# Seven block products for eight in two pairs of row tiles, and a batch's column term added by GpSimd

## The chip, the cores and the metric

The kernel runs on one core of one Trainium2 chip. The metric is device time in microseconds of one execution, from the start to the end on the chip. Names of the engines in the profile: PE is TensorE's matmul, PEld its weight load, DVE is VectorE, ACT is ScalarE, POOL is GpSimd, SP is the sync engine, which here issues most DMAs.

## What is computed

Two blocks follow each other, each with a residual. The input `x` is 2 x 1024 x 2048 in f32, the context is 2 x 2048 x 2048, the weight 2048 x 2048.

```python
def xattn(x1, x2):                       # x1: layer norm of x, x2: the context
    q1 = fake_quant(x1, x1_scale, x1_zp) # round, clip to 0..255, less zero point, times scale
    q2 = fake_quant(x2, x2_scale, x2_zp)
    return q1 @ q2
def ffn(x, weight):
    s = 127 / clip(max(abs(x), axis=-1), 1e-5)
    xq = clip(round(x * s), -128, 127) / s
    scale_w = 1 / clip(mean(abs(weight)), 1e-5)
    tw = clip(round(weight * scale_w), -1, 1)          # -1, 0 or 1
    return einsum('bsi,oi->bso', xq, tw) / scale_w
x = x + tanh(g_xattn) * xattn(layernorm(x), context)
x = x + tanh(g_ffn) * ffn(layernorm(x), weight)
```

## The kernel before

**Tiling.** Each of the two batches is eight row tiles of 128 rows, held as f32 in `resid` (eight buffers, so that a row of batch 1 takes the buffer of a row of batch 0 once that is stored). Each batch has a first product (rows by context) and a second one (rows by weight), each 8 tiles x 2048 x 2048. A matmul is 128 x 128 by 128 x 512; half a row tile (1024 columns) of one product is 32 of them.

**First product** (`first`, L611, added to the row by VectorE at L620). The row is normalized (bn_stats L378), quantized by ScalarE (L434), clipped by VectorE (L437) and transposed into `turned` or `tw`, by PE in batch 0 (L444, copies L450) and by DMA on the SP queue in batch 1 (L454). The context is quantized into the f16 store `ca` by ScalarE (L547), clipped by VectorE (L550) and summed by columns (L555, L557, then PE at L581). Since the quantized values are kept centred, the zero points leave a **column term** `colg` (one value for each column, made by `column_term`, L586) and a **row term** `rowg` (one value for each row, summed in batch 0 by GpSimd at L460 to L465 and ScalarE at L469, in batch 1 by ScalarE at L473). `terms` adds both to the row in one VectorE instruction, which also gives the row's sum for the mean:

```python
nc.vector.scalar_tensor_tensor(                                    # L640
    v, colg, rowg[:, t : t + 1], v, ALU.add, ALU.add, accum_out=acc[:, i : i + 1])
```

**Second product** (`norm2`, `norm2_tile`, `second`). From the sum come the mean (L668), the squares and their sum (ScalarE, L677), the largest square (VectorE, L684), a few small operations on two rows at a time (L690 to L704, the root on ScalarE at L697, the product's scale `am` at L708), the quantization (ScalarE, L748), a cast (VectorE, L757) and the transposition (PE at L762 with copies at L768 for one pair, DMA at L774 for the others). PE multiplies with the ternary weight in fp8 (L814), VectorE scales and adds (L823), and the half row is stored (L829), issued by GpSimd, for the last two rows by SP.

**Weight.** The 16 tiles of the weight are loaded twice (L854): once for the mean of absolute values (L865, scale at L874 to L883), once for the quantization by ScalarE (L899), the clip to fp8 by VectorE (L903) and the transposition into `tw`, by PE and a copy for the first six (L909, L913), by DMA for the others (L917).

**Order.** No instruction is placed by hand. Each piece of work is a step in a `Plan`, with engine, cost in us, due time, the keys that it reads and writes, and flags for buffers, DMA time and `port`. `Plan.order` simulates the steps, at each turn taking the one that can start first on its engine, with the due time as a tie-break; `Plan.latest` goes back from the end and gives new due times; after ten such rounds the best order is issued. Two steps with `port` do not overlap in this simulation; it stands for what VectorE and GpSimd share. Engines work through their instructions in the order issued. The rows are taken in the order 6, 7, 0, 1, 2, 3, 4, 5, in batch 1 as 14, 15, 8 to 13. PSUM has three buffers `mm` of 1024 f32 columns for the products, and two `tr`. Five buffers `turned` hold transposed rows of either product.

In batch 1 the first products are written as column half 0 of four rows, half 1 of the same, then both halves of each of the last four; the second products follow row by row. The planner mixes them.

Of the kernel before, what the change touches and what calls it, by code (L numbers as in the profile page):

```python
# [18 lines left out]
Q_EPS = 1e-5  # L19
# [4 lines left out]
class Plan:  # L24
# [128 lines left out]
    def give_out(self):  # L153
# [6 lines left out]
        due, best = [s[2] for s in steps], None  # L160
        for i in range(self.ROUNDS):
            order, ends, passed = self.order(due, follow, waits)
            if best is None or max(ends) < best[0]:
                best = (max(ends), order)
            due = self.latest(ends, passed, follow)
        for n, slot in best[1]:
            if slot is None:
                steps[n][3]()
            else:
                steps[n][3](slot)  # L170
# [3 lines left out]
def flamingo_gated_kernel(  # L174
# [69 lines left out]
    acc = const.tile([P, MT], F32, name="acc")  # L244
    rowg = const.tile([P, 2 * MT], F32, name="rowg")
# [46 lines left out]
    plan = Plan({"work": NWORK, "tp": NTP, "mm": 3, "tr": 2})  # L292
    step = plan.step
    aT, qT, pm = {}, {}, {}
    taken = {}

    def scalars():

        s = {}

        def spread(slot):
            s["pp"] = tr[slot]
            nc.tensor.matmul(s["pp"][:, 2:6], ones32[0:1, :], par1[:, 2:6], start=True, stop=True)
            nc.tensor.matmul(s["pp"][:, 0:2], ones32[0:1, :], tg1, start=True, stop=True)

        def of(i, rs, zc):
            nc.vector.reciprocal(rs, par[:, i : i + 1])  # L310
            nc.vector.tensor_scalar(zc, par[:, i + 1 : i + 2], CENTER, None, ALU.subtract)

        def rest():
            nc.vector.scalar_tensor_tensor(g1, par[:, 2:3], par[:, 4:5], tg[:, 0:1], ALU.mult, ALU.mult)
            nc.vector.scalar_tensor_tensor(g1d1, zc1, -1.0, g1, ALU.mult, ALU.mult)
            nc.vector.scalar_tensor_tensor(g1d2, zc2, -1.0, g1, ALU.mult, ALU.mult)
            nc.vector.tensor_scalar(kd2, zc2, -float(K), None, ALU.mult)
            nc.vector.tensor_scalar(gkd, kd2, g1d1, None, ALU.mult)

        step("ACT", 0.3, 0.0, lambda: nc.scalar.activation(tg1, par1[:, 0:2], AF.Tanh), wr=[("tg1",)], hold=4.0)  # L320
        by = step("PE", 0.6, 6.0, spread, rd=[("tg1",)], wr=[("pp",)], take="tr", hold=6.8)
        step(
            "DVE", 0.2, 6.0, lambda: nc.vector.tensor_copy(par, s["pp"][:, 0:6]), rd=[("pp",)],
            wr=[("par",)], give=[by],
        )
        step("DVE", 0.3, 6.1, lambda: of(2, rs1, zc1), rd=[("par",)], wr=[("p1",)])
        step("DVE", 0.3, 6.2, lambda: of(4, rs2, zc2), rd=[("par",)], wr=[("p2",)])
        step("DVE", 0.9, 10.0, rest, rd=[("p1",), ("p2",)], wr=[("g",)])

    def res(t):  # L330
        return resid[:, t % MT, :]

    def xk(t, h=None):
        return [("x", t % MT, i) for i in ((0, 1) if h is None else (h,))]

    strip = const.tile([P, 30 * 2 * MT], F32, name="strip")
    stats6 = const.tile([P, 4, K // 512, nc.vector.BN_STATS_DIM], F32, name="stats6")
    used = [0]

    def tiny(n=1):  # L340
        used[0] += n
        return strip[:, used[0] - n : used[0]]


    def load_x(t, due, queue, halves=1, hold=0.0):
        w = K // halves
        for h in range(halves):

            def bring(h=h):
                q = nc.sync if queue == "SP" else nc.gpsimd  # L350
                q.dma_start(out=res(t)[:, ts(h, w)], in_=xrow[t][:, ts(h, w)])

# [67 lines left out]
    def norm1_tile(t, due, by_pe, fold_it, place, pieces, ready, scales, on_dve):  # L420
# [5 lines left out]
        def quant(i, slot=None):  # L426
            if i == 0:
                s["q"] = work[:, slot, :]
# [696 lines left out]
```

## Time and profile before

| | us |
|---|---|
| median of 3 runs | 498.72 (497.08 to 500.88) |
| profiled execution, its own time | 496.74 |
| its span | 495.0 |
| PE busy | 467.6 (2422 instructions) |
| DVE busy | 340.6 |
| ACT busy | 276.6 |
| POOL busy | 63.5 |

The span is the time from the first to the last instruction of the profiled execution; busy times are shares of it. In the profile's lines L611 is line 611 of the kernel. A group's line gives the engine, the operation, written tile and read tiles, shape, count, then busy time and the mean of one in ns, then the idle time of the engine just ahead of those instructions and what ended it. By the chain of waits the first matmuls run from 25 us, the first product of batch 0 until about 146, its second product until 274, mixed at its end with batch 1's first product, whose last pieces lie at 427, and the rest is the second product of batch 1. Batch 0's eight L640 lie between 113 and 162, batch 1's between 346 and 432.

### The profile page before, as it was taken

The numbers are of one execution on the slowest core, as the hardware profiler recorded it, in microseconds if no ns is written. First come the engines' busy times: TensorE is split into PE (matmuls) and PEld (weight loads), VectorE is DVE, ScalarE is ACT, GpSimd is POOL, SyncE is SP. The second block draws the span as 40 slices with busy tenths as digits, with TensorE's granted clock in tenths as the row PEclk, the third lists the DMA queues.
The fourth block names the chain that finished last, engine by engine and source line by source line (L and its number), as shares of the span: only waits on it lengthen the run. The fifth ranks groups of instructions, "written<-read, shape, count | busy, mean of one in ns | idle before, by whom it ended". The sixth has DMA issues, their size and how long they took to land.

```text
span 495.0 us, 6179 instructions
## 1 busy us (share of the span) xinstructions
PE 467.6 (94%) x2422; PEld 223.0 (45%) x2422; DVE 340.6 (69%) x568; ACT 276.6 (56%) x258; POOL 63.5 (13%) x76
## 2 busy tenths in 40 slices
PE   0599999999998799999999999999999999999996
PEld 0244454444467344444444444444444444444442
DVE  4999989959999688556697957632989831572122
ACT  4997896878999988631488364530454430050000
POOL 0574529100000020100100100000000000000000
PEclk9999999999999899999999999999999999999999
DMA  8999968992189999999999995610041542215122
GB/s 293 425 419 424 366 214 338 428 407 81 60 215 366 260 301 295 306 258 330 402 363 341 297 269 189 100 28 1 0 66 47 144 111 102 86 61 153 79 92 85
DMA packets 76170, 108.94 MB, mean 220 GB/s; under 512 B 58220, under 2 KB 58220, under 8 KB 70892
## 3 DMA queue, kind: packets, MB, share of 16 engines
q1 hardware_dynamic: 72064, 93.86, 60.1%
q0 software_dynamic: 4064, 14.68, 7.7%
q8 instruction: 19, 0.31, 0.2%
q14 instruction: 11, 0.09, 0.1%
q10 hardware_dynamic: 12, 0.00, 0.0%
HBM read 77.59 MB, written 16.78 MB: 191 GB/s over the span
## 4 chain that ended last, share of the span: by engine, by line
PE 76%; DVE 14%; DMA 6%; issue 2%; ACT 1%; DVEq 0%
PE mm L814 40%; PE mm L611 32%; DVE resid L640 3%; DMA resid<-in_x_dram 2%; PE tr L814 2%; DVE strip L684 2%; DMA tw<-in_ctx_dram 2%; DVE resid L620 2%; DMA tw<-ca 2%; DVE stats L378 1%; DVE ca L550 1%; DVE ca L903 1%; ACT ca L547 1%; PE tr L444 1%; DVE colg L557 1%
## 5 line engine op out<-in xcount | busy, mean ns | idle before, releaser
L814 PE MATMUL mm<-tw,turned 128*128 128x512 fp8e4 (+1 forms) x1104 | 211.9, 353 | 4.7 <-DMA turned<-work 2.4
L611 PE MATMUL mm<-ca,turned 128*128 128x512 f16 x832 | 187.7, 384 | 0.5 <-DVE ca L550 0.3
L814 PEld LDWEIGHTS <-turned 128*128 128x128 f16 x1168 | 106.8, 98 | 122.7 <-issue 6.3
L611 PEld LDWEIGHTS <-turned 128*128 128x128 f16 x832 | 81.8, 99 | 99.0 <-issue 4.8
L823 DVE SCALAR_TENSOR_TENSOR resid<-mm,am,resid 128x1024 f32<-128x1024 f32 (+1 forms) x31 | 38.6, 1246 | 64.3 <-PE mm L814 64.2
L547 ACT ACTIVATE ca<-ca,scal 128x2048 int16<-128x2048 f32 (+1 forms) x30 | 50.5, 1692 | 36.9 <-DMA ca<-in_ctx_dram 36.4
L677 ACT ACTIVATE work<-resid,strip 128x1024 f32<-128x1024 f32 x32 | 36.4, 1138 | 57.8 <-DVE strip L668 54.1
L829 POOL DMA_DIRECT2D out_dram<-resid x30 | 18.1, 606 | 362.5 <-DVE resid L823 225.2
L620 DVE SCALAR_TENSOR_TENSOR resid<-mm,scal,resid 128x1024 f32<-128x1024 f32 x32 | 40.4, 1277 | 18.4 <-PE mm L611 18.2
L378 DVE BATCH_NORM_STATS2 stats<-resid 128x6 f32<-128x512 f32 x64 | 40.0, 678 | 7.9 <-DMA resid<-in_x_dram 7.9
L550 DVE TENSOR_SCALAR ca<-ca 128x2048 f16<-128x2048 int16 (+1 forms) x40 | 27.3, 698 | 24.5 <-ACT ca L547 24.5
L611 PE MATMUL mm<-ca,tw 128*128 128x512 f16 x192 | 43.1, 379 | 0.4 <-DVE tw L450 0.2
L748 ACT ACTIVATE work<-resid,strip 128x2048 int16<-128x2048 f32 x16 | 35.5, 2263 | 12.2 <-DVE strip L704 7.8
L684 DVE TENSOR_REDUCE strip<-work 128x1 f32<-128x1024 f32 x32 | 37.3, 1210 | 1.3 <-ACT work L677 1.3
L640 DVE SCALAR_TENSOR_TENSOR resid<-colg,rowg,resid 128x2048 f32<-128x2048 f32 x16 | 37.4, 2344 | 0.1
L434 ACT ACTIVATE work<-resid,strip 128x2048 int16<-128x2048 f32 (+1 forms) x17 | 33.4, 1984 | 1.3 <-DVE strip L400 1.3
L557 DVE TENSOR_TENSOR colg<-colg,ca 128x2048 f16<-128x2048 f16 x24 | 30.8, 1304 | 0.3
L611 PEld LDWEIGHTS <-tw 128*128 128x128 f16 x192 | 18.4, 98 | 22.8 <-DVE tw L450 0.7
L899 ACT ACTIVATE work<-ca,scal 128x2048 int16<-128x2048 f32 x13 | 25.6, 2005 | 1.6 <-DMA ca<-in_L_ffn_weight_dram 1.1
L473 ACT ACTIVATE work<-work,scal 128x2048 f16<-128x2048 f16 x8 | 16.0, 1994 | 18.5 <-DMA turned<-work 18.5
L865 ACT ACTIVATE tw<-ca 128x2048 int8<-128x2048 f32 x10 | 19.1, 1910 | 7.6 <-DMA ca<-in_L_ffn_weight_dram 7.5
L462 POOL TENSOR_TENSOR tw<-tw,work 128x512 f16<-128x512 f16 x16 | 21.8, 1364 | 1.6 <-DVE work L437 0.4
(93 smaller groups left out, 260.7 us busy)
## 6 DMA issues: line engine op xcount, KB each, us to landing
ca<-in_L_ffn_weight_dram SPq DMA_DIRECT2D x19, 1024.0 KB, 8.6
ca<-in_ctx_dram SPq DMA_DIRECT2D x16, 1024.0 KB, 12.3
resid<-in_x_dram SPq DMA_DIRECT2D x15, 1024.0 KB, 11.7
out_dram<-resid POOLq DMA_DIRECT2D x26, 512.0 KB, 3.8
tw<-in_ctx_dram SPq DMA_DIRECT2D x8, 1024.0 KB, 12.6
ca<-in_ctx_dram SPq DMA_DIRECT2D x14, 512.0 KB, 8.4
tw<-in_L_ffn_weight_dram SPq DMA_DIRECT2D x6, 1024.0 KB, 6.8
out_dram<-resid SPq DMA_DIRECT2D x3, 512.0 KB, 2.6
```

Source lines behind the costliest of these rows:

```text
L378: nc.vector.bn_stats(stats6[:, t % 4, c, :], res(t)[:, ts(c, 512)])
L434: nc.scalar.activation(d, v, AF.Identity, bias=bi, scale=sc)
L547: nc.scalar.activation(a.bitcast(I16), s["w"], AF.Identity, bias=zc2, scale=rs2)
L557: nc.vector.tensor_add(r, r, a2(kt - kt % 2, h * H, 2 * H))
L611: nc.tensor.matmul(pm[t][:, ts(q, U)], aT[t][:, kt, :], a2(kt, h * H + q * U, U), start=(kt == 0), stop=(kt == KT - 1),)
L620: nc.vector.scalar_tensor_tensor(v, pm[t], g1, v, ALU.mult, ALU.add)
L640: nc.vector.scalar_tensor_tensor(v, colg, rowg[:, t : t + 1], v, ALU.add, ALU.add, accum_out=acc[:, i : i + 1])
L677: nc.scalar.activation(s["dev", t, h], res(t)[:, ts(h, H)], AF.Square, bias=s["nm"][:, j : j + 1], accum_out=s["s2"][:, k : k + 1],)
L684: nc.vector.tensor_reduce(s["m2"][:, k : k + 1], s["dev", t, h], AX.X, ALU.max)
L748: nc.scalar.activation(s["q"].bitcast(I16).rearrange("p (k j c) -> p k j c", j=2, c=P), v.rearrange("p (k c j) -> p k j c", j=2, c=P), AF. ...
L814: nc.tensor.matmul(pm[t][:, o + b0 * P : o + b1 * P], qT[t][:, k, j, :], w8[:, k, j, b0 * P : b1 * P], start=(k + j == 0), stop=(k + j == PB),
L823: nc.vector.scalar_tensor_tensor(v, pm[t][:, 0 : n * U], am[:, t : t + 1], v, ALU.mult, ALU.add)
```

## The change

**Seven for eight.** For the last two pairs of rows in batch 1 (10 with 11, and 12 with 13), the second product of a pair is taken as a product of 2 x 2 blocks: a block row for each tile, the inner dimension and the columns cut in halves of 1024. `seven` does it with seven block products of 16 matmuls, over sums and differences of row blocks (`sums`, VectorE, f16) and differences of weight blocks (`weight_differences`, GpSimd, fp8, written where the context's column half 0 lay in `ca`). The parts accumulate in PSUM buffers x, y and z, and are added to the rows on the way (`take`), y being read and then accumulated further. The pairs before keep `second`.

**Terms of batch 0.** `terms` in batch 0 becomes four GpSimd additions of the column term, 512 columns each; the row's sum comes from the accumulator of the addition in `first` and from a new `column_sum`; the row term is left out until after the second product, where ScalarE adds it to each half row before the store.

**With it.** In batch 1 rows from the third on are normalized one by one (`alone`, `var_alone`, `scale_alone`), no more in pairs. The last four weight tiles are quantized by VectorE (`on_dve`). The last two rows' first products go half 0, half 0, half 1, half 1. The plan is made twice: all steps up to batch 1's products keep the due times found for the version without `seven`.

The body of the kernel moved into a function `build(SEVEN)`, which indents it; without that the core of the diff is:

```diff
         def add():
-            nc.vector.scalar_tensor_tensor(v, pm[t], g1, v, ALU.mult, ALU.add)
+            o = dict(accum_out=part_acc[:, 2 * t + h : 2 * t + h + 1]) if t < MT else {}
+            nc.vector.scalar_tensor_tensor(v, pm[t], g1, v, ALU.mult, ALU.add, **o)
...
+    def column_sum(due):
+        def go():
+            nc.vector.tensor_reduce(csum, colg, AX.X, ALU.add)
+            nc.vector.tensor_scalar(csum, csum, -1.0 / N, None, ALU.mult)
+        step("DVE", 2.45, due, go, rd=[("colg", 0), ("colg", 1)], wr=[("csum",)])
     def terms(t, due):
...
+        if t < MT:
+            for c in range(NQ):
+                step(
+                    "POOL", 1.3, due, lambda c=c: nc.gpsimd.tensor_add(v[:, ts(c, U)], v[:, ts(c, U)], colg[:, ts(c, U)]),
+                    rd=[("colg", c // 2)], wr=xk(t, c // 2), port=True,
+                )
+            return
...
         def mean(j, t):
+            if t < MT:
+                a = [part_acc[:, 2 * t + h : 2 * t + h + 1] for h in range(2)]
+                nc.vector.tensor_scalar(m, a[0], a[1], -1.0 / N, ALU.add, ALU.mult)
+                nc.vector.tensor_scalar(m, m, csum, None, ALU.add)
...
     def second(t, h, due, parts, pool="mm", last=False, apart=False):
...
+        if t < MT:
+            step(
+                "ACT", 0.3 + 0.45 * n, due + 2.0,
+                lambda: nc.scalar.activation(v, v, AF.Identity, bias=rowg[:, t : t + 1]),
+                rd=[("rowg", t)], wr=keys,
+            )
...
+    HK = PB // 2
+    def weight_differences(dues, engines):
+        for i, (due, by) in enumerate(zip(dues, engines)):
+            for q in range(2):
+                b11, b12, b21, b22 = w_part(q, 0), w_part(q + 2, 0), w_part(q, 1), w_part(q + 2, 1)
+                pair = ((b12, b11), (b22, t_part(0, q)), (b22, b12), (b21, t_part(1, q)))[i]
...
+                for c in range(PIECES[by]):
+                    def go(i=i, q=q, by=by, pair=pair, at=ts(c, w)):
+                        eng = nc.vector if by == "DVE" else nc.gpsimd
+                        eng.tensor_tensor(
+                            t_part(i, q)[:, at], pair[0][:, at], pair[1][:, at], ALU.subtract, saturate=False
+                        )
+                    step(
+                        by, w * (1.05e-3 if by == "DVE" else 2.35e-3) + 0.1, due, go, rd=rd, wr=[t_key(i, q)],
+                        port=True,
+                    )
+    PIECES = {"DVE": 4, "POOL": 8}
+    ENGINES = ("POOL",) * 4
+    def seven(pair, i, due, last):
...
+        def sums(n):
+            if n == 0:
+                nc.vector.tensor_add(s1, flat[u][:, 0:half], a22())
+            elif n == 1:
+                nc.vector.tensor_sub(s2, s1, a11())
+            elif n == 2:
+                nc.vector.tensor_sub(flat[u][:, 0:half], a11(), flat[u][:, 0:half])
+            else:
+                nc.vector.tensor_sub(s4, a12(), s2)
...
+        product("y", a11, lambda q: w_part(q, 0), lambda q: qt + W4(q, 0), due, start=True)
+        take("y", t, 0, due + d)
+        product("x", a12, lambda q: w_part(q, 1), lambda q: qt + W4(q, 0), due + d, start=True)
+        store(t, 0, take("x", t, 0, due + 2 * d, give=True), due + 2 * d)
+        product("y", lambda: s2, lambda q: t_part(1, q), lambda q: [keys[1]] + tk(1)(q), due + 2 * d)
+        take("y", t, 1, due + 3 * d)
+        product("z", lambda: s1, lambda q: t_part(0, q), lambda q: [keys[0]] + tk(0)(q), due + 3 * d, start=True)
+        take("z", u, 1, due + 4 * d)
+        product(
+            "y", lambda: flat[u][:, 0:half], lambda q: t_part(2, q), lambda q: [keys[2]] + tk(2)(q), due + 4 * d,
+        )
+        store(u, 1, take("y", u, 1, due + 5 * d), due + 5 * d)
+        product("z", lambda: s4, lambda q: w_part(q + 2, 1), lambda q: [keys[3]] + W4(q, 1), due + 5 * d)
+        store(t, 1, take("z", t, 1, due + 6 * d, give=True), due + 6 * d)
+        for q in range(2):
+            product(
+                "y", a22, lambda q: t_part(3, q), lambda q: qu + tk(3)(q), due + 6 * d, qs=(q,), give=give,
+            )
+            if last:
+                store(u, 0, take("y", u, 0, due + 7 * d, q == 1, q), due + 7 * d, q)
...
-        weight_quant(ot, place[ot], due, ot < 8 or ot % 2 == 1, ot > 5)
+        weight_quant(ot, place[ot], due, ot < 8 or ot % 2 == 1, ot > 5, ot >= 12)
...
-    plan.give_out()
+    plan, before = build(0)
+    due = plan.rounds()[0][:before]
+    plan, _ = build(2)
+    plan.give_out(plan.rounds(due)[1])
```

## The prediction

> **What bounds the kernel now.** I read the page first, then the chain of waits in order of time, then the timelines of the engines around the places where TensorE (PE) stands still. Busy share, granted clock and the chain's shares by engine:
>
> ```profile
> PE 467.6 (94%) x2422; PEld 223.0 (45%) x2422; DVE 340.6 (69%) x568; ACT 276.6 (56%) x258; POOL 63.5 (13%) x76
> ...
> PEclk9999999999999899999999999999999999999999
> ...
> PE 76%; DVE 14%; DMA 6%; issue 2%; ACT 1%; DVEq 0%
> ```
>
> PE is busy for 94% of the span at full clock but for one slice, and it holds 76% of the chain. DVE's 14% lies almost wholly before and in the handover from the first to the second product of batch 0. The chain in time (start, length, what):
>
> ```profile
> 161.37 7.80 DMA tw<-ca
> 169.17 0.14 issue
> 169.31 12.21 PE mm L814 x48
> ...
> 184.97 10.36 PE mm L814 x48
> ...
> 428.43 62.17 PE mm L814 x288
> 490.60 0.03 issue
> 490.63 0.75 DVE resid L823
> ```
>
> The last stretch is one unbroken row of 288 matmuls in 62.17 us: 215.9 ns for each, with nothing between. From 169 us on the chain is PE alone (column sums included), so there **a matmul less is 0.216 us less, as long as its operands come in time**. What else can move lies before: PE's timeline at the handover (start, length, and in brackets the idle time before it and its releaser):
>
> ```profile
> 153.60 2.85 PE L814 MATMUL mm<-tw,turned 128*128 128x128 fp8e4 x48 [2.35 <-DMA turned<-work]
> ...
> 163.36 3.61 PE L814 MATMUL tr<-tw,turned 128*128 128x512 fp8e4 x16 [1.10 <-ACT turned L768]
> 169.31 12.21 PE L814 MATMUL mm<-tw,turned 128*128 128x512 fp8e4 x48 [2.33 <-DMA tw<-ca]
> ```
>
> PE stands 2.35 + 1.10 + 2.33 = 5.78 us, and after the last gap 48 matmuls took 12.21 us where the same 48 took 10.36 us at 184.97: 1.85 us more, at a granted clock of 0.91 in the window 160 to 180. Together 7.63 us are there to be won or enlarged.
>
> **The seven products.** A pair of row tiles costs 8 block products of 16 matmuls now, 7 after the change; two pairs: 2 x 16 x 215.9 ns = **6.91 us off PE**, in the last stretch, where PE is the whole chain. The number of matmuls per weight load is unchanged. The end of the last matmul moves from 490.6 to about 483.7, and the two pairs take 2 x 7 x 3.454 = 48.4 us, so pair one begins near 435.3. By its order its third product (442.2) needs the first and second weight difference, the fifth (449.1) the third, the seventh (456.0) the fourth.
>
> **The weight differences.** New: 64 GpSimd subtractions of 512 fp8 elements, two inputs. No fp8 operation on GpSimd is in the trace. The nearest rows are the fp16 adds of 512 elements, two of them alone, the first undisturbed and the second beside VectorE's column adds (L557):
>
> ```profile
> 59.76 1.15 POOL L460 TENSOR_TENSOR tw<-work 128x512 f16<-128x512 f16 x1 [4.15 <-DVE work L437]
> ...
> 79.50 2.13 POOL L460 TENSOR_TENSOR tw<-work 128x512 f16<-128x512 f16 x1
> ```
>
> So the price lies between 1.15 and 2.13 us; the 24 adds of L460 and L462 took 11.9 + 21.8 = 33.7 us, 1.40 each, and I take that (same operation, same width, a like mix of neighbours). 64 x 1.40 = 90 us. They may start when all first products with column half 0 of batch 1 have passed. Those run from 260.9, with 32 matmuls of L814 and some 6 of column sums mixed in; half 0 of the last two rows is written after 12 units of 32 matmuls, so it is complete after 12 units if PE takes it early (384 + 38 matmuls, 352) and 14 units if it takes them as written (366). I take 359. Stores that GpSimd issues in between (8 x 0.53 for the four plain tiles, L829) add 4 us. The fourth difference ends at 359 + 90 + 4 = 453, 3 us ahead of 456. Cost **0, with little to spare**: the cover is the 55 us of plain products between. At 1.15 us it ends at 437; at 2.13 at 499, 43 us late.
>
> The Trainium skill, "SBUF — State Buffer", section "Who interferes with whom", speaks against this placing: a VectorE instruction with two SBUF inputs, or in a two-port mode, and a GpSimd instruction that reads SBUF exclude each other for the whole instruction. The pair of lines above agrees in kind (1.15 against 2.13). By that rule 64 x 1.15 would grow by five L640 of 2.34 us and eight casts of 0.69 us that lie after 359: 91 us, ending at 454, no other verdict than the mean row gives.
>
> **VectorE in the pairs.** Seven takes a pair instead of four, 1.28 each (L823): +3.8 us. Four sums of 1024 fp16 elements; L557 does 2048 in 1.30, so 0.65 each: +2.6 us. Six tiles are now normalized alone: 17 small operations a tile instead of 6, near 0.2 us each: 13 us over the stretch. By the windows VectorE is busy for 80 of the 155 us after 340; it would be for about 100 after the change, so it fits in sum. What it can cost is a late take, because the next product but one accumulates in the same buffer. The slack shows in
>
> ```profile
> 452.64 1.28 DVE L823 SCALAR_TENSOR_TENSOR resid<-mm,am,resid 128x1024 f32<-128x1024 f32 x1 [5.31 <-PE mm L814]
> 456.09 1.28 DVE L823 SCALAR_TENSOR_TENSOR resid<-mm,am,resid 128x1024 f32<-128x1024 f32 x1 [2.17 <-PE mm L814]
> 466.45 1.28 DVE L823 SCALAR_TENSOR_TENSOR resid<-mm,am,resid 128x1024 f32<-128x1024 f32 x1 [9.08 <-PE mm L814]
> ```
>
> the 2.17 us that VectorE waits between the adds of two units. A take behind one L640 (2.34 us) is late by 0.2, behind a sum held by a GpSimd operation (0.65 + 1.15) by nothing. Bounds 0 to 2 us (a few of 14 takes late by 0.2 to 0.5); **+0.5**.
>
> **The column term on GpSimd.** Eight additions L640 go from VectorE in batch 0 (8 x 2.34 = 18.7 us, all between 113 and 162, where it is busy without a break), 32 GpSimd adds of 512 f32 come (no f32 add there in the trace; bounds again 1.15 and 2.13, at 1.40: 5.6 us a tile, 45 in all), plus the accumulator reads (16 x 0.08), a reduce of the column term (two L684 of 1.21: 2.4 us) and a second small operation per mean. Net VectorE falls by some 14 us. GpSimd has been idle since 88, and the column term's half 0 is there at 103.1, so half 0 of the first tiles is hidden; half 1 is there at 113.1 and takes 2.3 to 4.3 us a tile against 2.34 now. The groups:
>
> ```profile
> L823 DVE SCALAR_TENSOR_TENSOR resid<-mm,am,resid 128x1024 f32<-128x1024 f32 (+1 forms) x31 | 38.6, 1246 | 64.3 <-PE mm L814 64.2
> ...
> L677 ACT ACTIVATE work<-resid,strip 128x1024 f32<-128x1024 f32 x32 | 36.4, 1138 | 57.8 <-DVE strip L668 54.1
> ...
> L640 DVE SCALAR_TENSOR_TENSOR resid<-colg,rowg,resid 128x2048 f32<-128x2048 f32 x16 | 37.4, 2344 | 0.1
> ...
> L462 POOL TENSOR_TENSOR tw<-tw,work 128x512 f16<-128x512 f16 x16 | 21.8, 1364 | 1.6 <-DVE work L437 0.4
> ```
>
> What is that worth at the handover? ScalarE (ACT) is as full as VectorE there: from 117.94 to 162.3 it idles 1.8 us, and its squares, quantizations and copies stay. But VectorE's queue did hold things up: ScalarE ended the quantization of a weight tile at 155.29,
>
> ```profile
> 153.25 2.04 ACT L899 ACTIVATE work<-ca,scal 128x2048 int16<-128x2048 f32 x1
> ```
>
> and VectorE, in an L640 begun 0.1 us before, clipped it only at 157.46:
>
> ```profile
> 155.19 2.34 DVE L640 SCALAR_TENSOR_TENSOR resid<-colg,rowg,resid 128x2048 f32<-128x2048 f32 x1
> ...
> 157.46 2.35 DVE L903 TENSOR_SCALAR ca<-work 128x2048 fp8e4<-128x2048 int16 x2
> ```
>
> These 2.2 us stand ahead of the weight transposes on the SP queue (issued from 158.74) that PE waited for at 169.3. They share the DMA with five weight loads issued at 150.1, so not all of it comes through. Bounds: a gain of 7.63 (all idle time and slow clock gone); a loss of 2.3 us, where at 2.13 us an add the third tile (three tiles of half 1: 113.1 + 3 x 4.26 = 125.9) is late for its second square, which ScalarE started at 123.59. Nearer to the single hold-up, half of which is hidden by DMA: **-1.0**.
>
> **The row term on ScalarE.** 16 activations of 1024 f32 at the end of batch 0, 1.14 each (L677): 18.2 us, less four weight quantizations of 2.0 us that go to VectorE (no f32 to int16 on VectorE in the trace: between 0.69, L757, and 2.34, L640; 1.22 as L903, 4.9 us in all). ScalarE is busy 76.8 of the 120 us from 160 to 280 and would be 87. Each store goes out some 1.2 us later, and with it the load of batch 1's row that reuses the buffer. Cost 0: PE never idles from 182 on, the last such row was transposed by about 322 and first products for others lasted to 373. If that cover were gone, it would be about 1.2 us once, plus a wait behind context quantizations that wait for DMA (up to 5 us each). I add **+0.5** for it and for VectorE waiting at GpSimd's adds.
>
> **Sum.** -6.91 + 0 + 0.5 - 1.0 + 0.5 = -6.9 us, on the profiled execution of 496.74 (span 495.0 and 1.74 around it): 489.8. That execution was 2.0 below the median of the runs, 498.72, which is what is predicted from: **491.8 us**. A measurement here tells about 1% (5 us) from no change.
>
> **Rivals.** *The handover closes* (0.13): VectorE's freed time lets weights and rows through early, PE does not stop and keeps its clock: 498.7 - 6.9 - 7.6 + 1.0 (the two terms of 0.5) = 485.2. For it: three waits, one traced to an L640. Against: ScalarE is as full, DMA too.
> *Given back* (0.26): the subtractions cost 1.56 each, so the fourth difference ends at 359 + 100 + 4 = 463 and the seventh product waits 7 us: 498.7. For it: only 3 us to spare, and VectorE's L640 and casts in that stretch. Against: PE may take half 0 early (352).
> *GpSimd becomes the bound* (0.19), the slower side: fp8 subtraction at 1.77, half way between mean and contended rows. 64 x 1.77 = 113, end at 476, 20 us late: 498.7 - 6.9 + 20 = 511.9. It decides the sign from 1.56 us on ((456 + 6.9 - 363) / 64) and makes the kernel slower by over 1% from 1.64 (5 us more). For it: nothing in the trace prices fp8 there. Against: 1.15 undisturbed, and no column adds (L557) this late.
> That the change does not do what it says would show as a matmul count that is not lower by 32.
>
> **Numbers.** The forecast (0.42) has its own range of 488 to 494.5. Faster by over 1% (below 493.7): nearly all of it and the first rival, 0.54. Within 1%: given back and the rest, 0.27. Slower: 0.19. The range leaves out most of the slow rival and the far end of the first: 485 to 502.
>
> **What would show it.** Right: PE's instructions down by 32; the last stretch an unbroken row ending near 484; POOL busy up by about 135 us (45 + 90) with a mean near 1.4; the fourth difference done before the seventh product; gaps between 150 and 170 of 3 to 6 us. Wrong: PE waits for POOL in the last 50 us (GpSimd is the bound), POOL means above 1.6, or gaps at the handover longer than 5.8 us.

## The result, and the profile after

The changed kernel takes **527.72 us** (median of 4 runs, 522.95 to 530.77) against 499.8 us for the kernel before, run beside it on the same chip: a ratio of 1.0569, with a 95% interval of 1.0437 to 1.0701. Forecast were 491.8 us in a range of 485 to 502. The profiled execution took 530.61 us with a span of 528.7; before the span was 495.0, so 33.7 us are to be found.

The page of the changed kernel, the rows that answer to those of before (busy time, granted clock by slice, the chain's shares):

```profile
PE 471.1 (89%) x2390; PEld 223.4 (42%) x2390; DVE 408.5 (77%) x662; ACT 287.6 (54%) x275; POOL 176.4 (33%) x172
...
PEclk9999999999969999999999989999999969989999
...
PE 36%; DMA 25%; DVE 25%; ACT 7%; issue 4%; SPq 2%; POOL 0%; DVEq 0%; ACTq 0%; POOLq 0%
```

The matmuls went down by 32 as they should, yet PE's busy time went up by 3.5 us: seven products took off 6.9, which by subtraction leaves 10.4 to the lower granted clock (two slices of 6 and two of 8, where before had a single 8). PE's share of the chain fell from 76% to 36%; VectorE's went from 14% to 25% and the DMA's from 6% to 25% (42 us of it are two loads of the context between 12 and 55 us, before most of the new work). **GpSimd, which has most of the new work, holds 0% of the chain.** PE's idle time (span less busy) rose from 27.4 to 57.6 us, by 30.2. By windows 4.7 of these lie before 60 us, 9.3 between 140 and 200, 2.1 near 310, and 13.7 between 420 and 500; the rest is spread. PE's timeline where it now stands longest in the last two stretches (start, length, and in brackets the idle time before it and its releaser):

```profile
152.36 1.04 PE L1138 MATMUL tr<-ident,ca 128*128 128x128 f16 x8 [8.83 <-DVE ca L1132]
...
430.12 27.28 PE L879 MATMUL mm<-tw,turned 128*128 128x512 fp8e4 x112 [7.37 <-DVE resid L888]
...
461.57 6.21 PE L1005 MATMUL mm<-tw,turned 128*128 128x512 fp8e4 x16 [4.17 <-DMA turned<-work]
...
487.17 3.46 PE L1005 MATMUL mm<-ca,turned 128*128 128x512 fp8e4 x8 [2.12 <-DVE resid L1028]
```

The three gaps of the handover (2.35, 1.10 and 2.33 before) have become one of 8.83, two of 2.36 and 2.97 and two small ones, and the last stretch, unbroken before, has three. All the lines shown but one name VectorE; the one that names a DMA waited for a row whose transposition was issued only after a late VectorE cast. So the next view is VectorE's timeline around these places:

```profile
127.94 1.28 DVE L637 SCALAR_TENSOR_TENSOR resid<-mm,scal,resid 128x1024 f32<-128x1024 f32 x1
...
129.14 1.22 DVE L721 TENSOR_REDUCE strip<-work 128x1 f32<-128x1024 f32 x1
130.27 11.55 DVE L748 TENSOR_TENSOR strip<-strip 128x2 f32<-128x2 f32 x1
...
407.54 18.39 DVE L674 SCALAR_TENSOR_TENSOR resid<-colg,rowg,resid 128x2048 f32<-128x2048 f32 x1
...
428.79 1.28 DVE L888 SCALAR_TENSOR_TENSOR resid<-mm,am,resid 128x1024 f32<-128x1024 f32 x1
...
445.59 11.04 DVE L821 CAST work<-work 128x2048 f16<-128x2048 int16 x2
...
476.52 9.40 DVE L989 TENSOR_TENSOR ca<-turned,ca 128x1024 f16<-128x1024 f16 x1
```

The first two lines are a product's addition and a reduction, as long as ever. Then comes an operation on 128 x 2 numbers with two inputs, 0.15 us elsewhere, that took **11.55**; an L674 (the former L640, 2.34 us undisturbed) that took 18.39; two casts of 0.69 that took 11.04; and a sum of `seven` that took 9.40 instead of 0.69. The line at 428.79 is the L888 that ended PE's wait at 430.12: it stood in VectorE's queue behind the instruction of 18.39 us. GpSimd's timeline at the same times:

```profile
114.76 27.05 POOL L668 TENSOR_TENSOR resid<-resid,colg 128x512 f32<-128x512 f32 x22 [1.14 <-DVE colg L602]
...
416.38 7.40 POOL L961 TENSOR_TENSOR ca<-tw 128x512 fp8e4<-128x512 fp8e4 x7
...
476.90 8.46 POOL L961 TENSOR_TENSOR ca<-tw,ca 128x512 fp8e4<-128x512 fp8e4 x8
```

The first line is 22 adds of the column term without a gap, from 114.76 to 141.81; VectorE's 11.55 us end at 141.82. The second is the last 7 of 16 differences that began at 406.90 and ended at 423.78; VectorE's L674 ended at 425.93, its own 2.1 us later. The third ended at 485.36, VectorE's sum at 485.92. The casts stood beside a row from 444.89 to 455.47. So **on each of these four held lines VectorE stood until a whole row of GpSimd instructions was over, not until the one that was running was over.** It was not so everywhere: an L674 at 387.65 waited for a single difference and took 3.18 us. The instructions that were held read two SBUF tensors or are casts between 16-bit types; the additions that read PSUM (L637, L888, L1028) and the reductions of one tensor (L721) ran beside the same rows at full speed.

GpSimd's own work was about as dear as forecast, or less (busy time and mean ns after the bar):

```profile
L961 POOL TENSOR_TENSOR ca<-tw 128x512 fp8e4<-128x512 fp8e4 x32 | 37.2, 1193 | 77.4 <-PE mm L627 77.4
...
L668 POOL TENSOR_TENSOR resid<-resid,colg 128x512 f32<-128x512 f32 x32 | 44.9, 1447 | 37.8 <-DVE colg L602 21.2
...
L961 POOL TENSOR_TENSOR ca<-tw,ca 128x512 fp8e4<-128x512 fp8e4 x32 | 34.6, 1108 | 0.1
```

The 64 differences cost 37.2 + 34.6 = 71.8 us, 1.12 each, where 1.40 was taken, and the 32 adds 1.45 where 1.40 was taken.

### The profile page after: what moved, and what is told of

Read it like the earlier page. It is cut to its first block, busy times and chain, and to the rows that moved or that the text cites. A ratio compares the mean times of both kernels' runs of the same rounds, so it can differ in the third digit from the quotient of the medians.

```text
span 528.7 us, 6360 instructions
## 1 busy us (share of the span) xinstructions
PE 471.1 (89%) x2390; PEld 223.4 (42%) x2390; DVE 408.5 (77%) x662; ACT 287.6 (54%) x275; POOL 176.4 (33%) x172
## 4 chain that ended last, share of the span: by engine, by line
PE 36%; DMA 25%; DVE 25%; ACT 7%; issue 4%; SPq 2%; POOL 0%; DVEq 0%; ACTq 0%; POOLq 0%
PE mm L627 18%; PE mm L1005 8%; DMA tw<-in_ctx_dram 8%; PE mm L879 7%; DMA ca<-in_ctx_dram 6%; DMA ca<-in_L_ffn_weight_dram 5%; DVE resid L674 4%; DMA resid<-in_x_dram 4%; DVE work L821 2%; DVE strip L748 2%; DVE strip L721 2%; DMA out_dram<-resid 2%; DVE ca L989 2%; ACT work L1128 2%; DVE resid L637 2%
## 5 line engine op out<-in xcount | busy, mean ns | idle before, releaser
L627 PE MATMUL mm<-ca,turned 128*128 128x512 f16 x832 | 191.5, 387 | 5.6 <-DVE resid L637 2.1
L879 PE MATMUL mm<-tw,turned 128*128 128x512 fp8e4 (+1 forms) x848 | 159.5, 350 | 12.7 <-DVE resid L888 7.4
L627 PEld LDWEIGHTS <-turned 128*128 128x128 f16 x832 | 82.0, 100 | 106.8 <-issue 10.4
L879 PEld LDWEIGHTS <-turned 128*128 128x128 f16 x912 | 83.6, 100 | 99.8 <-issue 17.2
L894 POOL DMA_DIRECT2D out_dram<-resid x26 | 15.3, 590 | 152.0 <-ACT resid L913 93.4
L961 POOL TENSOR_TENSOR ca<-tw 128x512 fp8e4<-128x512 fp8e4 x32 | 37.2, 1193 | 77.4 <-PE mm L627 77.4
L637 DVE SCALAR_TENSOR_TENSOR resid<-mm,scal,resid 128x1024 f32<-128x1024 f32 x32 | 40.9, 1279 | 22.4 <-PE mm L627 22.4
L668 POOL TENSOR_TENSOR resid<-resid,colg 128x512 f32<-128x512 f32 x32 | 44.9, 1447 | 37.8 <-DVE colg L602 21.2
L566 DVE TENSOR_SCALAR ca<-ca 128x2048 f16<-128x2048 int16 (+1 forms) x40 | 29.4, 744 | 16.2 <-ACT ca L563 16.1
L721 DVE TENSOR_REDUCE strip<-work 128x1 f32<-128x1024 f32 x32 | 38.1, 1212 | 4.1 <-ACT work L714 4.0
L674 DVE SCALAR_TENSOR_TENSOR resid<-colg,rowg,resid 128x2048 f32<-128x2048 f32 x8 | 35.6, 4455 | 0.0
L961 POOL TENSOR_TENSOR ca<-tw,ca 128x512 fp8e4<-128x512 fp8e4 x32 | 34.6, 1108 | 0.1
L888 DVE SCALAR_TENSOR_TENSOR resid<-mm,am,resid 128x1024 f32<-128x1024 f32 x22 | 28.1, 1277 | 8.1 <-PE mm L879 8.1
L1028 DVE SCALAR_TENSOR_TENSOR resid<-mm,am,resid 128x1024 f32<-128x1024 f32 (+1 forms) x15 | 18.0, 1208 | 17.0 <-PE mm L1005 17.0
```

Source lines behind the costliest of these rows:

```text
L627: nc.tensor.matmul(pm[t][:, ts(q, U)], aT[t][:, kt, :], a2(kt, h * H + q * U, U), start=(kt == 0), stop=(kt == KT - 1),)
L637: nc.vector.scalar_tensor_tensor(v, pm[t], g1, v, ALU.mult, ALU.add, **o)
L668: "POOL", 1.3, due, lambda c=c: nc.gpsimd.tensor_add(v[:, ts(c, U)], v[:, ts(c, U)], colg[:, ts(c, U)]),
L674: nc.vector.scalar_tensor_tensor(v, colg, rowg[:, t : t + 1], v, ALU.add, ALU.add, accum_out=acc[:, i : i + 1])
L721: nc.vector.tensor_reduce(s["m2"][:, k : k + 1], s["dev", t, h], AX.X, ALU.max)
L879: nc.tensor.matmul(pm[t][:, o + b0 * P : o + b1 * P], qT[t][:, k, j, :], w8[:, k, j, b0 * P : b1 * P], start=(k + j == 0), stop=(k + j == PB),
```

## The experiments

**Theory.** VectorE and GpSimd share something (call it the port), and while GpSimd has instructions ready one behind the other it keeps it; a VectorE instruction that needs it waits for the end of the row, and everything queued behind it on VectorE waits too. **Rivals**: VectorE is simply too full (408.5 us busy against 340.6); the new order of the plan is what costs; GpSimd's work collides instruction by instruction, each a little. In the kernel before, the folds (L460 to L465) each needed the one ahead, so no row of independent GpSimd instructions stood in it. Line numbers below shift by up to ten against the changed kernel's.

**One half at a time.** The first run keeps the changed terms of batch 0 and makes the plan without the seven products:

```diff
     plan, before = build(0)
-    due = plan.rounds()[0][:before]
-    plan, _ = build(2)
-    plan.give_out(plan.rounds(due)[1])
+    plan.give_out(plan.rounds()[1])
```

> Only the batch 0 half of the change: the column term on GpSimd, the row term on ScalarE, VectorE quantizing the last four weight tiles; the second product is eight block products everywhere, as before. Held-port theory (a VectorE instruction that needs the port shared with GpSimd waits for a whole row of back-to-back GpSimd instructions, not for one): the row of some 25 adds after 114 us stays, one small VectorE operation near 130 takes about 10 us, PE idles 10 to 16 us between 140 and 200 against 5.8 before, and the time is 508 to 516. Rival A (the loss lies in the seven products, VectorE's extra load there): 497 to 501. Rival B (the new plan's order is worse from the start, about 5 us more idle in the first 60 us whatever GpSimd does): 503 to 506, with the idle time before 60 us.

The second keeps the seven products, and has the terms of batch 0 and the quantization of the last weight tiles as before:

```diff
-            if t < MT:                  # terms: GpSimd's additions; mean and row term alike
+            if False:
...
-        weight_quant(ot, place[ot], due, ot < 8 or ot % 2 == 1, ot > 5, ot >= 12)
+        weight_quant(ot, place[ot], due, ot < 8 or ot % 2 == 1, ot > 5)
...
-        column_sum(60.0)
```

> Only the other half: seven products with the weight differences on GpSimd; batch 0's terms, means and weight quantization are on their engines as before. Held-port theory: no long VectorE instruction before 200 us and the start and handover of before; after 360 us single VectorE instructions of 8 to 18 us beside rows of differences, PE idle 10 to 16 us there and a few us of slow clock, against 6.9 us less matmul: 505 to 512. Rival A (the extra VectorE work of the pairs and of rows normalized alone is what costs): VectorE without gaps, no instruction above 3 us, 500 to 512. Rival C (each VectorE instruction waits at most for one GpSimd instruction, 1.1 us): 491 to 497.

Measured: 510.55 us for the terms alone (ratio 1.0227, 1.0146 to 1.0307) and 517.15 for the seven products alone (1.0345, 1.0268 to 1.0423), against 497.99 for the kernel before. So each half loses by itself, 2.3% and 3.5%, and the two add up to the 5.7% of the whole. The seven products alone lost more than the 505 to 512 us expected. VectorE's timeline with the terms alone:

```profile
126.64 11.60 DVE L748 TENSOR_TENSOR strip<-strip 128x2 f32<-128x2 f32 x1
```

and PE's, where it stood longest after the start:

```profile
148.77 1.03 PE L1138 MATMUL tr<-ident,ca 128*128 128x128 f16 x8 [8.83 <-DVE ca L1132]
```

VectorE's timeline with the seven products alone:

```profile
455.32 12.54 DVE L989 TENSOR_TENSOR ca<-turned,ca 128x1024 f16<-128x1024 f16 x1
```

and PE's behind it:

```profile
469.11 3.51 PE L1005 MATMUL mm<-ca,turned 128*128 128x512 fp8e4 x8 [5.26 <-DVE resid L1028]
```

The held subtraction of 128 x 2 and PE's 8.83 us come with the terms (the row of 22 adds is there from 111.16 to 138.22); the held sum (until 467.86, the row of GpSimd until 467.31) and PE's stand for the addition behind it come with the seven products. The order was planned anew in both, so as a cause it is not out yet.

Long holds are not all of the loss. With the seven products alone, the first row of differences (14 of them, on GpSimd's timeline) ran without a gap, and VectorE's small operations got through it one at a time, each about 1 us long instead of 0.16, as the line of VectorE shows:

```profile
349.61 14.79 POOL L961 TENSOR_TENSOR ca<-tw 128x512 fp8e4<-128x512 fp8e4 x14 [73.94 <-ACT work L714]
...
358.13 1.02 DVE L383 TENSOR_TENSOR strip<-strip 128x4 f32<-128x4 f32 x1
```

PE's longest wait for VectorE after the start came behind this stretch:

```profile
374.96 14.85 PE L627 MATMUL mm<-ca,turned 128*128 128x512 f16 x56 [7.58 <-DVE resid L637]
```

So the third rival, single collisions, has a part in this loss.

**The row broken up.** If the row is what holds, a wait inside it should let VectorE in. After each of the 96 GpSimd instructions a copy of one element of what it has just written is put, so that GpSimd's queue must wait for its own result; nothing is taken away:

```diff
                             eng.tensor_tensor(
                                 t_part(i, q)[:, at], pair[0][:, at], pair[1][:, at], ALU.subtract, saturate=False
                             )
+                            if by == "POOL":
+                                nc.gpsimd.tensor_copy(gap, t_part(i, q)[:, at][:, w - 1 : w])
...
+                        nc.gpsimd.tensor_add(w, w, colg[:, ts(c, U)])
+                        nc.gpsimd.tensor_copy(gap, w[:, U - 1 : U])
```

> The whole change, with one thing added: after each GpSimd add of the column term and each weight difference GpSimd copies one element of the result to a scratch column, which makes it wait for the add's end, so no two of these run back to back (96 copies of 128x1, some 0.1 to 0.3 us each, plus the waits). The modelled costs and so the order given out are those of the change. Held-port theory: VectorE gets in at every gap, no VectorE instruction is longer than its own time plus about 1.5 us, the sum of held time falls from about 45 us to 15, PE's idle time after 120 us falls from 25 to 8 us, and the time to 498 to 508 although GpSimd has 20 to 30 us more to do. Rival A (load) and rival B (order): within 1.5% of the change's 527.7 or slower.

The same 96 copies, but of a constant, so that there is as much GpSimd work and no wait:

```diff
-                                nc.gpsimd.tensor_copy(gap, t_part(i, q)[:, at][:, w - 1 : w])
+                                n = next(gaps)
+                                nc.gpsimd.tensor_copy(gap[:, n : n + 1], ones32[:, n : n + 1])
...
```

> The whole change with one-element copies as in the run with gaps, but each reads a constant tile and not the result of the instruction ahead of it, so GpSimd never waits between two instructions. If the port is handed over only when GpSimd's queue has to stop, VectorE is held through whole rows again (instructions of 9 to 18 us) and the time is 520 to 535. If the end of any instruction, or a copy between two large ones, is enough to let VectorE in, it is near the run with gaps: 497 to 505.

Measured: **499.59 us with the waits** (ratio 1.0027, 0.999 to 1.0065) and **529.19 without** (1.0645, 1.0591 to 1.07). In the traces a copy begins about 0.06 us after the instruction ahead of it ends in the first run, and 0.05 us before that in the second, so there it did not wait. GpSimd's busy time went up in both, from 176.4 to 205.7 and 193.7, and the one with more of it is 30 us faster. VectorE's timeline with the waits:

```profile
127.36 1.19 DVE L757 SCALAR_TENSOR_TENSOR strip<-strip 128x2 f32<-128x2 f32 x1
...
398.95 3.77 DVE L680 SCALAR_TENSOR_TENSOR resid<-colg,rowg,resid 128x2048 f32<-128x2048 f32 x1
```

GpSimd's beside it:

```profile
127.27 1.26 POOL L670 TENSOR_TENSOR resid<-resid,colg 128x512 f32<-128x512 f32 x1
...
400.63 2.14 POOL L971 CAST gap<-ca 128x1 f32<-128x1 fp8e4 x1
```

and VectorE's without the waits:

```profile
402.66 20.24 DVE L682 SCALAR_TENSOR_TENSOR resid<-colg,rowg,resid 128x2048 f32<-128x2048 f32 x1
...
442.57 12.16 DVE L829 CAST work<-work 128x2048 f16<-128x2048 int16 x2
```

With the waits VectorE's busy time fell from 408.5 to 376.0 us, and none of its instructions took over 3.77: a small one of 0.17 stood 1.19 until 128.55, for the one add that ran (127.27 to 128.53), and L680 of 2.34 took 3.77 (one difference, then its own time) while GpSimd's next copy, 0.18 otherwise, stood 2.14 until VectorE was through. So hand in hand the two exclude each other one instruction at a time; without a wait the same instruction, there L682, stood 20.24 us. Two rivals fall as causes of the 28 us. The order: the copies stand inside steps whose cost in the planner is unchanged, and the traces of the changed kernel and of both runs have the same instructions in the same order on every engine, apart from the copies. The load: with the waits VectorE has the same 662 instructions, and GpSimd more work. Single collisions are still there with the waits, and cost little.

The theory is too sharp, though. In the run without waits, VectorE's small operations in batch 0 got in at the end of each add, with GpSimd never pausing; here one of them, and the add on GpSimd that held it:

```profile
134.84 1.31 DVE L385 TENSOR_TENSOR strip<-strip 128x4 f32<-128x4 f32 x1
...
134.87 1.26 POOL L671 TENSOR_TENSOR resid<-resid,colg 128x512 f32<-128x512 f32 x1
```

Between 140 and 200 us PE idles 12.1 us with the waits and 13.5 without; some 21 of the 28 us are idle time of PE after 380, where the holds of 20.24 and 12.16 lie. Shown is that with a wait behind each GpSimd instruction no hold lasts much longer than one of them, and that without it VectorE is often, not always, kept out until the row ends. What decides between the two is open, and that it is a port in the hardware, and not something in the queue, is inferred.

**Where the 6.9 us went.** With the rows broken the whole change is worth nothing, no gain of seven. So the halves again, with the waiting copies, and the seven products with their differences on VectorE:

```diff
-    ENGINES = ("POOL",) * 4
+    ENGINES = ("DVE",) * 4
```

> Batch 0's half only, with the same one-element copies after each of the 32 GpSimd adds. Held-port theory: the 11 us instruction is gone, what is left is up to 1.2 us of waiting for each small VectorE operation with two inputs in SBUF: PE idles 6 to 11 us at the handover, 498 to 505 against 510.6 without the copies. If GpSimd's slower delivery of the rows is what costs, it stays at 508 to 513.

> Seven products only, batch 0 as before, the differences on GpSimd, each followed by a one-element copy of its result that waits for its end. Held-port theory: the run with the differences back to back (517.2) loses its waits: no VectorE instruction over 4 us, PE without a wait after 180 us but for 1 to 2 us, the handover as before, so the 6.9 us of matmuls come through nearly whole: 490 to 494, faster than the kernel before. If the seven products cost in another way (VectorE's load, late takes), 497 to 503 as with the differences on VectorE.

> Seven products only, batch 0 as before, and the weight differences on VectorE, 32 of 1024 elements in place of GpSimd's 64 of 512 (estimate from the f32 row of 128x1024 with two SBUF inputs, half of 2.34 us: 1.17 each, 37 us in all). Held-port theory: nothing is held; VectorE has about 140 us of work in the last 150, PE waits 0 to 6 us for late takes or late differences: 492 to 499. Rival A (VectorE's load in the pairs is what made the change slow): 37 us more on VectorE makes it worse than the change's own last part, over 510.

Measured: the terms alone, with waits, 505.26 us (ratio 1.0172, 1.0128 to 1.0217); the seven products alone, with waits, 497.37 (1.0005, 0.9967 to 1.0042); with the differences on VectorE 499.2 (1.0011, 0.9968 to 1.0054). The last has 39 us more work on VectorE (32 subtractions of 1.22) and loses nothing against the kernel before, which speaks against VectorE's load in this half too. The seven products with waits missed the 490 to 494 us expected, so the waits remove this half's 3.5% but bring no gain. The terms of batch 0 lose with the waits too (1.7% against 2.3%; the two intervals overlap): PE still stood 5.69 us for the clipped weight tile at 145.75. Which part of this half costs that (32 adds that each hold small VectorE instructions, the weight quantization moved to VectorE, or the order) was not told apart.

The seven products with waits do take 8.4 us off PE (459.2 busy against 467.6), and from 374 us on PE does not stop at all. The whole change with waits (1.0027) is also 7 us faster than the terms alone with waits (1.0172), about what the 32 matmuls are worth, though in another order. But with the seven products alone PE's idle time is 35.2 us against 27.4. The longest new gap, in PE's timeline, is far from the pairs:

```profile
262.81 1.03 PE L628 MATMUL mm<-ca,turned 128*128 128x512 f16 x4
267.22 6.18 PE L628 MATMUL mm<-ca,turned 128*128 128x512 f16 x20 [3.39 <-DMA turned<-work]
```

This is the joint of the two batches: the new plan puts a first product of batch 1 ahead of the last 16 matmuls of batch 0's second product, and its transposed row landed 3.39 us late. In the kernel before, 16 matmuls of the second product stood at this place and PE ran through:

```profile
263.37 3.62 PE L814 MATMUL mm<-tw,turned 128*128 128x512 fp8e4 x16
```

The run with the differences on VectorE has the same gap, 3.51 us.

**The order at the joint.** Theory A: the gain is given back at this joint. Theory B: it is eaten all along, by GpSimd's contention. Three other ways to plan the same kernel: each engine's order in batch 0 chained to that of the plan without the seven products, with the differences on GpSimd (waits kept) and on VectorE, and one plan without kept due times:

```diff
+    for n, _ in order:                      # the two chained plans
+        if n < batch0:
+            engine = plan.steps[n][0]
+            if engine in last:
+                plan.steps[n][4].add(last[engine])
+            last[engine] = n
...
-    plan.give_out(plan.rounds(due)[1])      # the free plan
+    plan.give_out(plan.rounds()[1])
```

> The seven products with GpSimd's differences and the waiting copies, batch 0's terms as in the kernel before, and each engine's order of batch 0's steps chained to the order that the plan without the seven products gives. Theory A (the 6.9 us do come off PE in the pairs, and were given back where the new order put a first product of batch 1 ahead of its transposed row at the joint of the batches): that wait of 3.4 us is gone or under 1 us, PE's idle time returns from 35 to 28 to 30 us, span near 489 to 491, time 490 to 493, ratio 0.985 to 0.99. Theory B (what is given back comes from GpSimd's adds themselves, as contention all along the last 130 us): idle time stays near 35 us, spread over many places after 360, time 496 to 498.

> The seven products with the weight differences on VectorE instead of GpSimd (no GpSimd work late), batch 0's terms as before, and batch 0's order chained to that of the plan without the seven products. Theory A (order at the joint): the joint's wait is gone, but VectorE carries some 18 us more; 492 to 496, ratio about 0.99, with PE waits on VectorE of 1 to 2 us between 370 and 430. Theory B (contention with GpSimd is what eats the gain): without any GpSimd row it should be the fastest of the three, 489 to 492.

> As the kernel with the seven products, waiting copies and batch 0's terms as before, but planned in one go with no due times kept from the plan without the seven products. Theory A (order at the joint): a different order at the joint, the wait of 3.4 us there goes or moves; 490 to 496, ratio 0.985 to 1.0 depending on where the new order puts it. Theory B (contention): 496 to 498, idle time near 35 us spread after 360 whatever the order.

Measured: 524.61 us, 524.61 and 505.83 (ratios 1.0534, 1.0539 and 1.016). All three missed both expectations. The chained plan let loads of the context pass the last transpositions of the weight on the SP queue (the last one was issued at 216.41 us, and at 194.20 in the kernel before), and PE stood for it, once. Its timeline in the first of the three:

```profile
225.71 8.86 PE L880 MATMUL mm<-tw,turned 128*128 128x512 fp8e4 x32 [21.70 <-DMA tw<-ca]
```

In these two runs nothing was held and PE ran unbroken from 240 us to the end; of the 26 us lost, 21.70 and 21.94 lie in this one wait of batch 0. The free plan, 7.5 us slower than the kernel before, has a wait of 8.69 for ScalarE's quantization of a weight tile (175.96). That shows what an order is worth here, and it speaks against theory B: the differences on GpSimd (with waits) and on VectorE give the same time, and neither makes PE stop in the last 280 us.

So only what the planner takes for a transfer at the joint was changed. In the plan with the seven products, a transposition of a row of batch 1 is taken to be 2 us longer (3 in a second run). PE's order stays as it was up to the joint, and there the last 16 matmuls of batch 0 move ahead; behind it the order changes as well, PE's here and there up to 392 us:

```diff
                     "SP", 1.3, due, turn_dma, rd=q_keys, wr=[("aT", t, 0), ("aT", t, 1)], take="tp",
-                    dma=3.8, port=None,
+                    dma=3.8 + (2 if SEVEN and t >= MT else 0.0), port=None,
```

> The kernel with the seven products, the waiting copies and batch 0's terms as before, planned with a transposition of a row of batch 1 taken as 2 us longer; all that stands ahead of the joint of the batches keeps its order, and at the joint the last unit of the second product of batch 0 (16 matmuls, 3.45 us) now stands ahead of the first product of batch 1 that waited 3.39 us. Theory A (the 6.9 us were given back at the joint only): no wait there above 0.5 us, PE idle about 31 us, span 490 to 491.5, time 492 to 494, ratio about 0.99. Theory B (what is given back is not tied to the joint): PE waits as long at some other place, time 496 to 498.

> The same with 3 us in place of 2: at the joint 12 matmuls of the first row instead of 8 ahead of the second row's. Theory A: as the run with 2 us, 492 to 494. Theory B: 496 to 498.

Measured: **493.58 us (ratio 0.9905, 0.9864 to 0.9947)** and 494.35 (0.9946, 0.9911 to 0.9981), against 497.25 for the kernel before. The page's row of PE with 2 us:

```profile
PE 459.6 (93%) x2390; PEld 218.6 (44%) x2390; DVE 372.1 (76%) x648; ACT 277.7 (56%) x261; POOL 155.0 (31%) x204
```

and PE's timeline at the joint:

```profile
239.75 29.73 PE L880 MATMUL mm<-tw,turned 128*128 128x512 fp8e4 x137
271.36 28.88 PE L628 MATMUL mm<-ca,turned 128*128 128x512 f16 x133 [1.88 <-DMA turned<-work]
```

Both beat the kernel before, by 1.0% and 0.5%, and the changed one. The first lies in the range expected of theory A, the second just above it. The gap at the joint was 1.88 us in this execution, not under 0.5 as expected, and none in the second run's; after it PE runs unbroken to the end of the span at 492.5. PE's idle time is still 32.9 against 27.4 us; by windows 1.9 of that lie at the joint, 1.9 in the first 110 us and 1.1 at the handover. The medians fit theory A in part: 3.7 and 2.9 us of the 6.9 are kept. That it is the one gap of 3.39 us that gave them back is not shown. The order behind the joint moved with it, and single executions differ by as much: the second run's profiled one (498.88 us) has no gap at the joint, but waits 4.97 us in the handover where the first, in the same order, waits 2.75.

## Why the prediction was wrong, point by point

- **Seven products, -6.91: right.** 32 matmuls fewer, and PE's busy time fell by 8.4 us with the seven products alone (with waits), at least what the count gives. As time it came through only in part, 3.7 us in the best order.
- **Weight differences, 0: the prices were right, the cost was not.** 1.12 us each instead of 1.40, and PE never waited for them. The step asked only when GpSimd would be ready and not what GpSimd does to VectorE meanwhile. They did not end by 453 either, but at 490.90: GpSimd's own stores of finished rows wait for VectorE's additions, and these were late.
- **VectorE in the pairs, +0.5 (bounds 0 to 2): the step that failed most.** It took "a sum held by a GpSimd operation (0.65 + 1.15)" to make a later addition late by nothing, and one L640 ahead of it by 0.2. A sum took 9.40, an L674 18.39, two casts 11.04. Idle time between 420 and 500 came to 13.7 us, and the clock fell with it. The bound was one GpSimd instruction; it should have been a whole row of them, and the sixteen independent ones of each difference stood plainly in the diff.
- **Column term, -1.0 (bounds -7.63 to +2.3): wrong in sign and outside its bounds.** The freed 14 us of VectorE were counted, and the hold of 11.55 by the last ten of 22 adds in a row was not. This half alone, with the row term and the weight quantization in it, cost 2.3% (11 us); in the whole change 9.3 us of idle time lie between 140 and 200, and a gap of 8.83 at the handover, one of the prediction's own signs of being wrong (over 5.8). With the waits this half still cost 1.7%, so the long hold is not shown to be its main cost; the rest stays open.
- **VectorE waiting at GpSimd's adds, inside the last +0.5: the same fault.** It was named, and priced by one add.
- **The lines shown of before could not carry the bound.** The pair 1.15 and 2.13 us at L460 was read as the whole range of what the two engines do to each other. These adds depend on each other, so GpSimd stopped after each; the trace held no row of independent GpSimd work beside a two-input VectorE instruction.
- **The rule.** The Trainium skill, "SBUF — State Buffer", section "Who interferes with whom", lets whichever of the two starts first keep the pair for the whole instruction. The prediction used it to lengthen GpSimd's work, which gave 91 us and no harm. The runs with waits agree with it (1.19 us for one add), and so do stretches of those without (1.02 us at 358.13); other rows go beyond it, with 9 to 20 us for a row.
- **The slower rival** had the sign and, with 511.9 (its terms add up to 511.8), part of the size, but the wrong mechanism: it took GpSimd as the bound, at 1.77 us a difference. GpSimd was fast and nobody waited for its results. The rival that was missing is "GpSimd's row holds VectorE".
- **The order.** "The end of the last matmul moves" took for granted that the rest of the plan stays. With the holds gone, PE stood at new places, the longest 3.39 us at the joint, some 170 us ahead of the pairs, and two changed plans gained 3.7 and 2.9 us.
- Not settled: 4.7 us more idle time before 60 us in the changed kernel's execution, where VectorE's order differs slightly from before. Two other runs in the same order had 1.9 and 3.2 there, so part of it is this execution.

## What to carry to other kernels

Before work goes to an idle GpSimd, list the VectorE instructions beside it that read two SBUF tensors or cast between SBUF tensors, and let the upper bound for each be the whole run of independent GpSimd instructions, not one; a queue behind such an instruction (here the additions that free PSUM) is late by as much. A short GpSimd instruction that depends on the one before it breaks the run for 0.2 us and here gave back 28 us. And a gain on the bounding engine is not in hand until the joints of the new order have been read for gaps: here 2 us in the planner's model of one transfer lay between a ratio of 1.0005 and one of 0.9905 (3 us: 0.9946).

## What the runs showed of the hardware that was not expected

- A VectorE instruction of 0.15 us on 128 x 2 numbers stood 11.55 us beside a run of GpSimd adds; a row's L674 18.39, where 2.34 is usual. Whatever the two share was handed over each time GpSimd's queue waited, and often not between instructions that were ready: 499.59 against 529.19 us with the same number of copies. In other rows it was handed over after each instruction (1.02 us at 358.13 with the seven products alone, 1.31 at 134.84 with the copies that do not wait); what decides is not known.
- Beside the same runs, VectorE's additions with one operand in PSUM (1.28 us) and its reductions of one f32 tensor (1.22 us) were not slowed.
- GpSimd's fp8 subtraction of 512 elements took 1.08 us undisturbed, its f32 add 1.27. On VectorE the same subtraction took 1.22 us for 1024 elements.
- A copy of one element on GpSimd took 0.18 us, and with the wait for the result ahead of it the step from one difference to the next grew from 1.05 to 1.30 us.
